# Left sums three steps earlier, and a softmax's exps moved within the last batch of a graph layer

## The chip, the cores and the metric

The kernel runs on one core of a Trainium2 chip. The metric is the device time of one execution in microseconds; the median of several runs counts. The core has five engines with queues of their own: TensorE (PE, matrix products), VectorE (DVE), ScalarE (ACT), GpSimd (POOL) and SyncE (SP), which here issues the DMAs.

## The reference

Sixteen graphs (batches) of 1024 nodes with 512 features pass through two layers over one 1024 x 1024 matrix adj. Cut to what matters:

```python
# layer 0
h = relu(layernorm(x))
x = x + (adj @ h) @ W0 + bias
# layer 1, graph attention
u = relu(layernorm(x)); h = u @ W
e = leaky_relu(s1[:, :, None] + s2[:, None, :]) * adj   # s1 = h.a1, s2 = h.a2
att = softmax(e, axis=2)
x = x + elu(att @ h + beta * h)
```

Everything is float32. The kernel takes s1 and s2 straight from u, with the vectors W.a1 and W.a2.

## The kernel before

**Products.** Each large product is done as a 2 x 2 block product with seven block products instead of eight, p1 to p7 (table `PRODUCTS`), with sums of blocks on both sides. In layer 0, from batch 1 on, six of the seven (all but p7) are split once more in the same way, into seven inner products r1 to r7 of half the size: 128 x 128 weights, 256 columns moving. `products_a2` writes out the order by hand. An inner product needs sums of its left operand: `inner_left` makes them on DVE with four adds of 128 x 256. The first of them (`s[:, 0]`) is the weight of r5, the second of r6, the fourth of r3; the third add changes the operand in place for r7. In the trace these sums are `in_p`, the operands `h` and `hS`, and the outputs `y_p3y`, `y_p3x` (the inner banks of p3) and `y_Y`, `y_X`, `y_W` (the outer PSUM banks). ACT copies r1, r5 and r7 out of PSUM, DVE adds r6 and then the whole to the outer bank (`y_p5t`, `y_p3t` and so on are these temporaries).

**Steps.** The order around this is a plan by hand. A batch of layer 0 is cut into steps: 0 to 6 hold p1 with p2, 7 to 13 p6 with p5, 14 to 20 p3 with the plain p7, 21 to 27 p4 with the first of the products with W0 (`po_Y`). Then `layer0_b` runs the other products with W0 with its own step numbers, two for each product, 2 to 13. After each step the plan's calls for that step are recorded, and every engine executes its own instructions strictly in the order in which they were recorded. Beside the products of batch b the plan does the norm of batch b + 1 (`h_stats`, `h_relu`) and what follows batch b − 1: its second norm (`o.stats`, `o.relu`), the stores of x (`x1d`) and u (`ud`), and `o.logits`, two multiply-and-sum instructions on DVE for each 128 rows of u. `o.store_logits` ends with a small DVE transpose of s2 over a tile `s2t` that POOL first clears. `load_res` fetches the residual rows (`xr`) for the current batch.

**The first softmax.** Batch 0's attention for layer 1 is begun inside layer 0. In batches 5 to 12 the masked logits are made, one row block g at a time, and stored to DRAM (`ed`). In the last batch of layer 0 (b = 15) they come back and are finished, by two plans of letters, `FIRST_A` (steps 0 to 27) and `FIRST_B` (steps of `layer0_b`): `Rg` reloads block g (512 KB, tile `er`), `Eg` takes its exp on ACT in four instructions, `Vg` turns it on DVE in two block transposes, `B` and `b` take buffers for the result, `S` and `s` send the sums through DRAM to all partitions (`sd`, `sall`), `D` and `d` put the diagonal in, `T1` and `T2` are block sums for layer 1's products. Steps 0 and 1 of the second plan are run at steps 23 and 26 of the first.

**Buffers.** Pool `b4` has 12 slots of 4 KB per partition. The inner sums, the temporaries, the outer sums, `er` and `e` tiles all live there. Pool `stat` gives two slots to most tags; PSUM has eight banks.

All engine calls go through the class `InOrder`, so every instruction of the profile has its line, L115; tiles tell them apart.

Of the kernel before, what the change touches and what calls it, by code (L numbers as in the profile page):

```python
# [29 lines left out]
F32 = mybir.dt.float32  # L30
# [4 lines left out]
P = 128  # L35
Q = 32
# [29 lines left out]
def kernel(  # L66
# [12 lines left out]
    B, N, D = x.shape  # L79
# [14 lines left out]
    stat = ctx.enter_context(tc.tile_pool(name="stat", bufs=2))  # L94
# [12 lines left out]
    class InOrder:  # L107


        def __init__(self, engine):  # L110
            self.engine = engine
# [5 lines left out]
    pe, dve, act, pool, sp = (  # L117
        InOrder(e) for e in (nc.tensor, nc.vector, nc.scalar, nc.gpsimd, nc.sync)
    )
# [217 lines left out]
    class Weighted:  # L337
# [9 lines left out]
        def steps(self, n, left):  # L347

            prod, _, bn, kind, first, last = self.products[n]

            def step(q, i, dc):
                if first and i == 0 and dc == 0:
                    self.banks[kind, q] = bank(f"{self.name}_{kind}{q}")
                ps = self.banks[kind, q].rearrange("p (i o) -> p i o", i=2)
                pe.matmul(
                    ps[:, i, :], left[:, dc, ts(2 * q + i, P)], self.w[:, W_BLOCK[bn], dc, :],
                    start=(first and i == 0 and dc == 0), stop=(last and dc == 1),
                    skip_group_check=True,
                )
                if i and dc:  # L360
                    self.done(prod, q, ps)

            return [partial(step, q, i, dc) for q in range(2) for i in range(2) for dc in range(2)]
# [261 lines left out]
    class LayerOut:  # L625
# [3 lines left out]
        def __init__(self, b):  # L629
            self.b = b  # L630
            self.us = {}
            self.norms = {}
            x1d[b] = dram.tile([2, 2, P, 2 * D], F32, name=f"x1d_{b}")
            names = ("U00", "U01", "U10", "U11")
            ud[b] = {n: dram.tile([P, 1024], F32, name=f"ud_{b}_{n}") for n in names}
            s1d[b] = dram.tile([P, NCH], F32, name=f"s1d_{b}")
            s2d[b] = dram.tile([G, Q * Q], F32, name=f"s2d_{b}")
            self.s12 = stat.tile([P, 2, NCH], F32, tag="s12", name=f"s12_{b}")

        def keep(self, nh, q):  # L640
            xr = xrs[self.b, nh, q]
            sp.dma_start(out=x1d[self.b][nh, q], in_=xr.rearrange("p k d -> p (k d)"))
# [27 lines left out]
        def store_logits(self):  # L670

            b = self.b
            sp.dma_start(out=s1d[b], in_=self.s12[:, 0, :])
            s2t = stat.tile([P, 2, Q], F32, tag="s2t", name=f"s2t_{b}")
            pool.memset(s2t[:, 0, :], 0.0)
            dve.tensor_copy(s2t[:, 0, 0:NCH], self.s12[:, 1, :])
            dve.transpose(s2t[:, 1, :], s2t[:, 0, :])
            sp.dma_start(out=s2d[b].rearrange("s (g q) -> (s g) q", q=Q), in_=s2t[:, 1, :])
# [426 lines left out]
    def plan_out(o, b):  # L1105

        return steps(
            (-1, o.keep, 0, 1), (-1, o.keep, 1, 0), (-1, o.keep, 1, 1), (0, o.stats, 0, 1, 0),
            (1, o.stats, 1, 0, 0), (2, o.relu, 0, 0), (3, o.stats, 1, 0, 1),
            (4, o.stats, 0, 1, 1), (7, o.relu, 1, 0), (8, o.relu, 0, 1), (9, o.stats, 1, 1, 0),  # L1110
            (10, o.stats, 1, 1, 1), (11, o.relu, 1, 1),
            (3, o.store, 0, 0), (8, o.store, 1, 0), (9, o.store, 0, 1), (12, o.store, 1, 1),
            (0, inner_left, b, "p6"), (1, inner_left, b, "p5"),
            (3, o.logits, 0, 0, 0), (4, o.logits, 0, 0, 1), (8, o.logits, 1, 0, 0),
            (9, o.logits, 1, 0, 1), (10, o.logits, 0, 1, 0), (11, o.logits, 0, 1, 1),
            (13, inner_left, b, "p3"), (15, o.logits, 1, 1, 0), (16, o.logits, 1, 1, 1),
            (16, o.store_logits), (18, inner_left, b, "p4"),
            (10, load_res, b, 0, 0), (13, load_res, b, 0, 1), (15, load_res, b, 1, 0),
            (18, load_res, b, 1, 1),
        )  # L1120
# [28 lines left out]
    def plan_softmax(order, s):  # L1149
# [35 lines left out]
        13: {9: "N n"},  # L1185
    }
    FIRST_A = {
        1: "R0", 4: "R1", 7: "B E0 V0 R2", 10: "E1 V1 R3", 12: "R4", 15: "E2 V2", 18: "b R5",
        22: "R6",
    }  # L1190
    FIRST_B = {
        0: "E3 V3 S", 1: "E4 V4 R7", 3: "E5 V5", 4: "E6 V6", 6: "E7 V7 s", 7: "D", 9: "T1a",
        10: "T1b", 11: "d", 12: "T2a", 13: "T2b",
    }
    LOADS_U = {5: ("U00",), 7: ("U01",), 9: ("U10", "U11")}

# [2 lines left out]
    out_of = None  # L1199
    for b in range(B):  # L1200
        plans = [plan_out(out_of, b)] if b else []
        plans_b = [plan_bias(b)]
        if b + 1 < B:
# [105 lines left out]
```

## Time and profile before

| | us |
|---|---|
| three runs | 2328.81, 2331.11, 2330.7 |
| their median | 2330.7 |
| the profiled execution | 2327.41 |
| its span, first to last instruction | 2325.6 |

The profile is of one execution, and its durations are summed against that execution's own 2327.41 us. The chain of waits that ended last lies for 81% on PE:

```profile
PE 81%; ACT 7%; DVE 7%; DMA 3%; issue 2%; SPq 1%; POOL 0%; DVEq 0%; ACTq 0%; POOLq 0%
```

Layer 0 takes the first half: its last products with W0 end at 1155.7 us. In a row of waits stand the engine and the tile it was to write, what it waited for, the total in us, the number of times and the longest. In a timeline row stand the start, the time until the last of a merged group ended (matmuls overlap, so that this is longer than the step to the next start), the engine, the operation and the tiles. The work of the reloaded blocks, from the view of the tile er (least, median and longest duration in ns, first and last start in us):

```profile
L115 ACT ACTIVATE er<-er,nm x32: 492/495/514, 1094.5 to 1144.6; 128x256 f32<-128x256 f32 x32
L115 DVE STREAM_TRANSPOSE pT<-er x16: 669/684/712, 1096.6 to 1145.8; 128x512 f32<-128x512 f32 x16
```

That is 32 exps of some 495 ns on ACT and sixteen block transposes of some 684 ns on DVE, between 1094.5 and 1146.5 us.

### The profile page before, as it was taken

The page shows a single profiled execution, that of the slowest core. Times are in us where ns is not written, and L with a number is a line of the kernel's source. Part 1 is how long each engine was busy: PE and PEld are TensorE (multiplying, and loading weights), DVE is VectorE, ACT ScalarE, POOL GpSimd, SP SyncE. Part 2 cuts the span into 40 slices and gives each one's busy share as a digit, 9 for nine tenths or more (in the row PEclk, how much of TensorE's full clock was granted, in tenths as well). Part 3 has the DMA queues.
Part 4 walks back from the last instruction along what each step waited for, and adds up shares of the span by engine and source line. Part 5 has one row for each costly group of instructions (what it writes and reads, how often), then busy time and mean ns, then how long its engine had stood idle before and what let it go on. Part 6 is the DMA issues. An engine that isn't in the chain of part 4 may idle for free.

```text
span 2325.6 us, 29418 instructions
## 1 busy us (share of the span) xinstructions
PE 2276.7 (98%) x8344; PEld 1587.3 (68%) x8344; DVE 1865.1 (80%) x4101; ACT 1544.3 (66%) x4147; POOL 529.3 (23%) x680
## 2 busy tenths in 40 slices
PE   9999999999999999999999999999999999999998
PEld 5787778877778877788755666556665466655565
DVE  7877787887888877877988788888988888878774
ACT  3766667666776667676367767677676776767753
POOL 1332222332232323122101222022220122201220
PEclk9999999999999999999999999999999999999999
DMA  6334343343343343433554545555456443455441
GB/s 213 126 129 150 123 155 122 135 137 121 134 158 128 125 144 111 145 126 122 173 168 146 164 135 168 183 162 166 138 167 190 154 155 115 147 186 160 136 128 37
DMA packets 194291, 336.02 MB, mean 144 GB/s; under 512 B 78800, under 2 KB 86992, under 8 KB 194128
## 3 DMA queue, kind: packets, MB, share of 16 engines
q1 hardware_dynamic: 193808, 333.61, 44.1%
q8 instruction: 66, 1.08, 0.2%
q14 instruction: 97, 0.79, 0.1%
q10 hardware_dynamic: 320, 0.52, 0.1%
HBM read 228.33 MB, written 109.91 MB: 145 GB/s over the span
## 4 chain that ended last, share of the span: by engine, by line
PE 81%; ACT 7%; DVE 7%; DMA 3%; issue 2%; SPq 1%; POOL 0%; DVEq 0%; ACTq 0%; POOLq 0%
PE z_Y L115 15%; PE y_Y L115 10%; PE po_Y L115 10%; PE pq_Y L115 8%; PE z_X L115 7%; PE po_X L115 5%; PE pq_X L115 4%; PE z_W L115 4%; PE y_W L115 3%; ACT xr L115 2%; PE po_W L115 2%; PE y_X L115 2%; PE pq_W L115 2%; ACT junk L115 2%; PE y_p1y L115 2%; PE y_p4y L115 2%
## 5 line engine op out<-in xcount | busy, mean ns | idle before, releaser
L115 POOL TENSOR_TENSOR x<-x,r 128x512 f32<-128x512 f32 x120 | 198.9, 1674 | 883.7 <-DVE x L115 325.3
L115 ACT ACTIVATE e<-e,nm 128x256 f32<-128x256 f32 x480 | 237.2, 498 | 140.5 <-DVE nm L115 140.5
L115 DVE CUSTOM_DVE_ANT_0 e<-e,mask 128x256 f32<-128x256 f32 x512 | 226.4, 498 | 105.8 <-DMA mask<-maskd 88.3
L115 PE MATMUL z_Y<-pT,ul_U 128*128 128x512 f32 x512 | 224.9, 592 | 0.0
L115 ACT ACTIVATE e<-s2b,s1b 128x256 f32<-128x256 f32 x512 | 216.5, 501 | 0.0
L115 POOL TENSOR_TENSOR xr<-xr,bias_bc 128x512 f32<-128x512 f32 x128 | 163.1, 1295 | 222.6 <-DVE xr L115 190.1
L115 PE MATMUL po_Y<-w_c,y_C 128*128 128x256 f32 x768 | 188.3, 379 | 0.0
L115 PEld LDWEIGHTS z_Y<-pT,ul_U 128*128 128x128 f32 x512 | 97.4, 190 | 115.5 <-issue 110.4
L115 PE MATMUL pq_Y<-w_c,z_C 128*128 128x256 f32 x768 | 174.4, 380 | 0.4 <-ACT z L115 0.4
L115 DVE CUSTOM_DVE_ANT_0 junk<-xr,v_bc 128x512 f32<-128x512 f32 x240 | 166.0, 692 | 6.8
L115 PEld LDWEIGHTS pq_Y<-w_c,z_C 128*128 128x128 f32 x768 | 145.6, 190 | 28.3 <-issue 7.6
L115 PE MATMUL y_Y<-adjT_B,h 128*128 128x512 f32 (+1 forms) x332 | 160.1, 596 | 1.6 <-ACT adjT_B L115 1.6
L115 PEld LDWEIGHTS po_Y<-w_c,y_C 128*128 128x128 f32 x768 | 146.1, 190 | 20.1 <-issue 0.5
L115 DVE STREAM_TRANSPOSE pT<-e 128x512 f32<-128x512 f32 x240 | 155.6, 687 | 1.0
L115 ACT ACTIVATE h<-x,nb_h,r_h 128x512 f32<-128x512 f32 (+1 forms) x132 | 98.2, 792 | 50.5 <-POOL nb_h L115 50.4
L115 ACT ACTIVATE junk<-xr 128x512 f32<-128x512 f32 x120 | 75.6, 630 | 70.4 <-DVE xr L115 69.9
L115 PE MATMUL po_X<-w_c,y_S 128*128 128x256 f32 x512 | 115.7, 379 | 0.0
L115 PE MATMUL pq_X<-w_c,z_S 128*128 128x256 f32 x512 | 115.6, 379 | 0.0
L115 PE MATMUL z_Y<-pT_T,ul_U 128*128 128x512 f32 x256 | 113.3, 594 | 2.1 <-DVE pT_T L115 1.9
L115 PE MATMUL z_W<-pT,ul_U 128*128 128x512 f32 x256 | 112.5, 592 | 0.0
L115 PE MATMUL z_Y<-pT_T,ul_S 128*128 128x512 f32 x256 | 112.5, 592 | 0.0
L115 PE MATMUL z_X<-pT_T,ul_S 128*128 128x512 f32 x256 | 112.5, 592 | 0.0
(227 smaller groups left out, 5056.0 us busy)
## 6 DMA issues: line engine op xcount, KB each, us to landing
mask<-maskd SPq DMA_DIRECT2D x128, 512.0 KB
x<-in_x_dram SPq DMA_DIRECT2D x64, 512.0 KB
xr<-in_x_dram SPq DMA_DIRECT2D x256, 128.0 KB
x1d<-xr SPq DMA_DIRECT2D x64, 512.0 KB
ul_U<-ud_U SPq DMA_DIRECT2D x64, 512.0 KB
x<-x1d SPq DMA_DIRECT2D x64, 512.0 KB
out_dram<-x SPq DMA_DIRECT2D x252, 128.0 KB
ud_U<-xr SPq DMA_DIRECT2D x60, 512.0 KB
```

The source lines that it names most:

```text
L115: return lambda *args, **kwargs: tc.keep_in_program_order(f(*args, **kwargs))
```

## The change

`inner_left` of p3 is called after step 10 instead of 13, and the logits that stood at 10 and 11 go to 12 and 13. The tile `s2t` is taken, and cleared by POOL, when the batch's `LayerOut` object is made instead of in `store_logits`. `FIRST_A` and `FIRST_B` get other steps: the reloads begin at step 11 instead of 1, the exps at 14 instead of 7, and the last five blocks come from step 22 on. The sum over blocks 0 to 3 (`S`) goes from step 23 to 24, that over 4 to 7 (`s`) stays at 6 of the second plan; `D` and the block sums `T1a` to `T2b` come one or two steps earlier.

```diff
@@ LayerOut.__init__ @@
             self.s12 = stat.tile([P, 2, NCH], F32, tag="s12", name=f"s12_{b}")
+            self.s2t = stat.tile([P, 2, Q], F32, tag="s2t", name=f"s2t_{b}")
+            pool.memset(self.s2t[:, 0, :], 0.0)
@@ LayerOut.store_logits @@
             sp.dma_start(out=s1d[b], in_=self.s12[:, 0, :])
-            s2t = stat.tile([P, 2, Q], F32, tag="s2t", name=f"s2t_{b}")
-            pool.memset(s2t[:, 0, :], 0.0)
+            s2t = self.s2t
             dve.tensor_copy(s2t[:, 0, 0:NCH], self.s12[:, 1, :])
@@ plan_out @@
             (3, o.logits, 0, 0, 0), (4, o.logits, 0, 0, 1), (8, o.logits, 1, 0, 0),
-            (9, o.logits, 1, 0, 1), (10, o.logits, 0, 1, 0), (11, o.logits, 0, 1, 1),
-            (13, inner_left, b, "p3"), (15, o.logits, 1, 1, 0), (16, o.logits, 1, 1, 1),
+            (9, o.logits, 1, 0, 1), (10, inner_left, b, "p3"), (12, o.logits, 0, 1, 0),
+            (13, o.logits, 0, 1, 1), (15, o.logits, 1, 1, 0), (16, o.logits, 1, 1, 1),
             (16, o.store_logits), (18, inner_left, b, "p4"),
@@ plans of the first softmax @@
     FIRST_A = {
-        1: "R0", 4: "R1", 7: "B E0 V0 R2", 10: "E1 V1 R3", 12: "R4", 15: "E2 V2", 18: "b R5",
-        22: "R6",
+        11: "R0", 12: "R1", 14: "B E0", 15: "V0 R2", 16: "E1", 17: "V1 E2", 18: "V2", 20: "b R3",
+        22: "E3", 23: "V3 R4", 24: "S", 25: "E4", 26: "V4 R5",
     }
     FIRST_B = {
-        0: "E3 V3 S", 1: "E4 V4 R7", 3: "E5 V5", 4: "E6 V6", 6: "E7 V7 s", 7: "D", 9: "T1a",
-        10: "T1b", 11: "d", 12: "T2a", 13: "T2b",
+        2: "E5 R6", 3: "V5 E6 R7", 4: "V6", 5: "E7", 6: "V7 s D", 7: "T1a", 8: "T1b", 11: "d T2a",
+        12: "T2b",
     }
```

## The prediction

> **What bounds the kernel now.** I read the page's busy shares, the waits of TensorE (PE), the waits of VectorE (DVE), then the timeline and the windows of the one place that the waits name. First the page:
>
> ```profile
> PE 2276.7 (98%) x8344; PEld 1587.3 (68%) x8344; DVE 1865.1 (80%) x4101; ACT 1544.3 (66%) x4147; POOL 529.3 (23%) x680
> ```
>
> PE is the bound; only 2325.6 − 2276.7 = 48.9 us of the span has it idle. Its waits, then the two of DVE's that matter:
>
> ```profile
> PE y_p3x L115 <- DVE in_p L115: 28.4, 15, 2.0
> PE y_p5y L115 <- DVE y_p5t L115: 4.6, 1, 4.6
> ```
> ```profile
> DVE s2t L115 <- POOL s2t L115: 38.3, 15, 3.0
> ...
> DVE y_X L115 <- ACT y_p5t L115: 13.9, 15, 0.9
> ```
>
> The reader is to see one wait, y_p3x on in_p, once in each of the 15 batches that use inner products, and one of 4.6 us that occurs once. PE's timeline in one such batch:
>
> ```profile
> 607.58 1.03 PE L115 MATMUL y_p3y<-adjT_B,hS 128*128 128x256 f32 x4
> 610.62 1.14 PE L115 MATMUL y_p3x<-ext,in_p 128*128 128x256 f32 x4 [2.02 <-DVE in_p L115]
> 611.56 3.58 PE L115 MATMUL y_Y<-adjT_B,h 128*128 128x512 f32 x4
> 614.98 1.03 PE L115 MATMUL y_X<-ext,hS 128*128 128x256 f32 x4
> ```
>
> The starts count. Undisturbed, four 128x256 matmuls take 0.865 us and the four of y_Y 1.72. From p3y to y_Y are 3.98 us where 1.73 are due: 2.25 lost. From y_Y to y_X are 3.42 where 1.72 are due: another 1.70 lost, while PE counts as busy. The windows say why (PEclk is the third value from the right):
>
> ```profile
> 607.00:611.00 4.00, 1.98 (x10) 1.46 (x9) 3.04 (x8) 3.22 (x7) 0.00 (x0) 1.00 0.53 188
> 611.00:615.00 4.00, 4.00 (x9) 1.86 (x8) 3.31 (x10) 3.11 (x11) 0.00 (x0) 0.57 0.89 206
> 615.00:619.00 4.00, 4.00 (x16) 2.79 (x15) 1.19 (x4) 3.87 (x13) 1.13 (x4) 1.00 0.06 9
> ```
>
> After the gap the clock falls to half for some 3.4 us. The steps between successive y_p3x starts show how often: 69.55 us without, 71.25 with. From 116.97 to 1036.47 there are 13 steps, 919.5 us in all = 13 × 69.55 + 9 × 1.70: 9 of 14 batches pay it. So the wait costs more than the 28.4 us of its row.
>
> Why in_p is late, on DVE:
>
> ```profile
> 607.24 0.69 DVE L115 TENSOR_TENSOR y_Y<-y_Y,y_p6t 128x512 f32<-128x512 f32 x1
> 608.85 1.30 DVE L115 TENSOR_TENSOR y_X<-y_X,y_p5t 128x512 f32<-128x512 f32 x2 [0.93 <-ACT y_p5t L115]
> 610.06 0.42 DVE L115 TENSOR_TENSOR in_p<-hS 128x256 f32<-128x256 f32 x1
> ...
> 616.99 0.17 DVE L115 COPY s2t<-s 128x8 f32<-128x8 f32 x1 [2.57 <-POOL s2t L115]
> ```
>
> in_p stands behind both y_X adds, which wait for ScalarE (ACT).
>
> **What the Trainium skill says.** "TensorE: Matmul & The Clock Gate", "What's actually happening": the array's clock runs full or half, decided by activity in a free-running window of about 3.4 us. The trace agrees in factor, length and in that only some gaps are hit; it disagrees in that the page wants an idle window, whereas gaps of 2.02 us suffice here. The trace decides. The same page, "Architectural detail": ACT and DVE are strict FIFO; the trace agrees (in_p behind y_X), so moved work must be checked by what is queued behind it. "Trainium Kernel Development and Optimization", "Key Constraints": all queues' DMAs share 16 engines; the reload er_7, issued at 1137.36 behind two ul loads, lets its exp start only at 1143.08.
>
> **The change part by part.**
>
> *Left sums of p3 (15 batches).* No instruction is added. In DVE's order the four adds of in_p take the place of the logits of (0,1,0) ahead of y_p5t: 610.06 to 611.52 = 1.46 us against 602.78 to 604.14 = 1.36. So y_p5t, y_p6t and y_Y keep their times within 0.1. In the built program in_p waits on no buffer, and p3x no longer on DVE. Saved in each of batches 1 to 14: 2.25 us; 14 × 2.25 = 31.5. The half-clock stretches go with their cause: 9 × 1.70 = 15.3.
>
> *What is late next.* I moved PE's starts in this batch 3.95 us earlier and followed the queues. The logits now stand after y_X (ends 610.06): three pairs at 1.46 reach 614.4, s2t 614.8, y_p3t reads its bank by 615.2. PE's next matmuls on that bank come at 616.2: 1.0 us spare. y_X of p3 needs ACT's copy, done by 610.15, PE comes at 611.02: 0.9 spare. ACT has its four norm sums (6.7 us) and a relu before the second y_p3t copy, now done at 620.0, 2.8 us after PE; DVE's y_X adds and sums then end at 626.1, y_p4t at 626.5, while PE's overwrite is at 627.4: 0.9 spare. ACT's idle stretches in p4 (2.5 and 5.2 us) absorb the lag, and by po_X all engines stand to PE as before. DVE is busy 57.2 us of a 71.25 us batch, so 67.3 hold it. Taken: 0 new wait; bounds 0 and 1 us per batch.
>
> *s2t earlier.* POOL's memset moves to the start of the batch; a POOL op of 0.12 us in an idle stretch. DVE's stall of 38.3 / 15 = 2.55 us is off PE's path now, so I count 0 for it, but it is cover for the first part: with it, y_p3t would end near 617.2 and PE would wait 1.0 us, 14 us in all.
>
> *The first softmax in batch 15.* From the p6 to the p4 starts are 1125.45 − 1090.89 = 34.56 us; undisturbed pieces of other batches add up to 12.08 (666.75 to 678.83) + 1.73 + 11.18 (1037.41 to 1048.59) = 24.99. So 9.57 us are lost now: 4.65 for y_p5t behind the exps and turns of er_0 and er_1, 0.5 for y_p5t's copy, the rest mostly at half clock (0.55 granted from 1107 to 1114). In the new order both turns leave the stretch before y_p5t, so that one runs as in other batches and p3y can start at 1102.98 (1090.89 + 12.08). I then placed each queue on that time:
>
> ACT: er_0 to er_2 (step 14 on) fill the place of the norm sums, which this batch lacks: 3 × 1.97 = 5.9 us for 6.7, from 1106.8 to 1112.7, in time for the second y_p3t copy (PE done 1112.6). Their reloads, 512 KB each, pass behind ud stores and xr loads on SP: er_0 can be issued by 1101.5 at the latest and er_1 at 1103.8, after the store that waits for a relu; about 4 us later they are there, er_1 (needed 1108.8) with least to spare.
>
> DVE: y_X ends at 1105.5, two logit pairs 1108.4, er_0's turn 1110.1 (1.30, and er_0's exps end at 1108.8), a pair 1111.55, s2t 1111.95, y_p3t 1112.35; PE is due at its bank at 1111.6: wait 0.8. Two more turns and p4's sums later DVE ends p3's sums at 1123.5; er_3's turn comes ahead of y_p4t, which reads its bank by 1125.2, PE due at 1123.7: wait 1.5.
>
> SP: er_5 to er_7 now stand behind sd_0, which waits for er_3's last exp (about 1121.4), the sall loads (4.4 us after sd now) and two more ul loads. From 1128.5 there are 5 × 0.5 MB queued; at the 350 GB/s of the busiest slices here they land at about 1134.5, 1136 and 1137.5. Their turns stand ahead of the xr adds that free the po banks: waits of 0.2, 0.4 and 1.0 us.
>
> Sum of waits 3.9; saved 9.57 − 3.9 = 5.6 (rounded down). Bounds: 9.5 with no new wait, −4 if the reloads come 10 us later. What is late next there: sd_1 follows er_7's exps, so the next softmax's s1b and s2b loads end near layer 1's first product instead of 3 us before it; ACT takes z_W first and DVE reaches the masks later, so no PE wait. T2, needed 13.7 us into layer 1, is ready some 6 us before.
>
> *Sum*, against the profiled execution's own 2327.4 us: 31.5 + 15.3 + 5.6 = 52.4, giving 2275.0. The median of the runs, 2330.7, is 3.3 above it, about what two more half-clock stretches would be; as these should vanish, I take no correction: 2275.
>
> **The rivals.**
>
> *New waits in p3 and p4.* The three margins of 0.9 to 1.0 us rest on one batch; if one is short by 1 us everywhere: 2275 + 14 = 2289. Against: PE has no other repeated wait now.
>
> *The half clock stays.* If it were not the gap that triggers it: 2275 + 15.3 = 2290. Against: I find it only beside a wait.
>
> *The tail of batch 15.* Reloads stacked behind sd_0 cost 10 us more, PE idle and once at half clock: 2287. For: they are issued later by whole steps, with 2.5 MB queued in one go.
>
> *The wait stays*, because p3x also waits for a bank or ACT: 2327. Against: its one other wait is on PE itself.
>
> *Slower.* in_p's four adds now stand ahead of y_p5t, whose read PE needs at 605.85 while it ends at 604.56: 1.3 us spare. Anything that holds the first add (a b4 buffer not yet free at step 10, where C12, C22 and three sums share 12) is a PE wait beyond 1.3. It decides when the hold passes 3.3 us: 2.0 of wait and 1.7 at half clock in 14 batches are the 52.4 gained. At 6 us: 14 × (4.7 + 1.7) − 52.4 = +37, so 2365. For: in the order of the built program another store's wait has moved onto the first add of p6's sums. Against: no semaphore on that add.
>
> **How the numbers follow.** Forecast 0.62; new waits 0.12; half clock 0.06; tail 0.14; wait stays 0.02; slower 0.04. The likeliest alone spans 2268 to 2281 (batch 15 from +9.5 to 0, runs within about 2). With the three rivals of the same sign: 2268 to 2291, which leaves out about a tenth. A difference of 0.2% (4.7 us) is about what a measurement can tell. Faster 0.94, same 0.02, slower 0.04.
>
> **What would show it.** Right: no y_p3x row among PE's waits; y_p3x steps of 67.3 us; PEclk 1.00 through p3; DVE's s2t row gone; in batch 15 PE waits of 1 to 2 us at p3y and p4y instead of 4.65 at p5y. Wrong: a y_p3y, y_X or y_p4y row 14 times; half clock without a gap; long PE waits on po banks after 1125.

## The result, and the profile after

| | before | after |
|---|---|---|
| median of 4 runs each, us | 2329.76 | 2276.76 |
| lowest and highest, us | 2326.34, 2331.11 | 2274.24, 2277.8 |
| the profiled execution, us | 2327.41 | 2277.24 |
| its span, us | 2325.6 | 2275.2 |

The changed kernel takes 0.9773 of the time (95% interval 0.9756 to 0.979), 53.0 us less. 2275.0 had been forecast, with a range of 2268 to 2291.

First the page of the changed kernel, its busy shares:

```profile
PE 2254.3 (99%) x8344; PEld 1578.3 (69%) x8344; DVE 1863.5 (82%) x4101; ACT 1540.7 (68%) x4147; POOL 526.6 (23%) x680
```

PE is now idle for 2275.2 − 2254.3 = 20.9 us of the span; it was 48.9. Its busy time also fell, by 22.4 us, with the same 8344 matmuls: matmuls at half clock count as busy, and 15.3 us of it are the nine stretches behind p3x. Next two rows of PE's waits (total, times, longest), and one of DVE's:

```profile
PE y_p4y L115 <- DVE y_p4t L115: 1.6, 1, 1.6
PE y_p3y L115 <- DVE y_p3t L115: 1.5, 1, 1.5
```
```profile
DVE y_p3t L115 <- ACT y_p3t L115: 35.8, 14, 2.6
```

The row of y_p3x on in_p, 15 times 2.0, is gone, and so are y_p5y's 4.6 and DVE's 38.3 us at s2t. From batch 1 to the end of layer 0 PE keeps only the two single waits shown, both in batch 15. DVE has a new repeated wait, for ACT's second copy of p3, which no PE row answers to. The timeline of PE in the batch that corresponds to the one shown before:

```profile
586.52 1.03 PE L115 MATMUL y_p3y<-adjT_B,hS 128*128 128x256 f32 x4
587.39 1.03 PE L115 MATMUL y_p3x<-ext,in_p 128*128 128x256 f32 x4
588.25 1.88 PE L115 MATMUL y_Y<-adjT_B,h 128*128 128x512 f32 x4
589.97 1.03 PE L115 MATMUL y_X<-ext,hS 128*128 128x256 f32 x4
```

The starts are 0.87, 0.86 and 1.72 apart: no idle time and full speed. The window of the same stretch has PE busy throughout, at a granted clock (third value from the right) of 1.00:

```profile
587.00:591.00 4.00, 4.00 (x16) 2.79 (x15) 3.22 (x9) 3.19 (x9) 0.00 (x0) 1.00 0.74 226
```

From batch 1 to batch 14 the 13 steps between successive y_p3x starts are 67.30 us (one is 67.35). They took 919.5 us before and take 991.24 − 116.29 = 874.95 now. The difference, 44.55, is 13 × 2.25 + 9 × 1.70 to the hundredth.

### The profile page after: what moved, and what is told of

The parts are those of the page before. It is cut to its first block, busy times and chain, and to the rows that moved or that the text cites. A ratio compares the mean times of both kernels' runs of the same rounds, so it can differ in the third digit from the quotient of the medians.

```text
span 2275.2 us, 29359 instructions
## 1 busy us (share of the span) xinstructions
PE 2254.3 (99%) x8344; PEld 1578.3 (69%) x8344; DVE 1863.5 (82%) x4101; ACT 1540.7 (68%) x4147; POOL 526.6 (23%) x680
## 4 chain that ended last, share of the span: by engine, by line
PE 86%; DVE 5%; DMA 4%; ACT 2%; SPq 1%; issue 1%; POOL 0%; DVEq 0%; ACTq 0%; POOLq 0%
PE z_Y L115 15%; PE y_Y L115 11%; PE po_Y L115 10%; PE pq_Y L115 8%; PE z_X L115 7%; PE po_X L115 5%; PE y_X L115 5%; PE pq_X L115 4%; PE z_W L115 4%; PE y_W L115 3%; PE po_W L115 2%; PE pq_W L115 2%; PE y_p1y L115 2%; PE y_p5y L115 2%; PE y_p6y L115 2%; PE y_p2y L115 2%
## 5 line engine op out<-in xcount | busy, mean ns | idle before, releaser
L115 PE MATMUL y_Y<-adjT_B,h 128*128 128x512 f32 (+1 forms) x332 | 147.2, 554 | 0.9 <-DVE adjT_B L115 0.9
L115 PE MATMUL z_X<-pT,ul_S 128*128 128x512 f32 x256 | 112.5, 592 | 0.0
```

Of the source, the lines that this page charges most:

```text
L115: return lambda *args, **kwargs: tc.keep_in_program_order(f(*args, **kwargs))
```

## The experiments

Each run was timed against the kernel before on the same chip. "Layer 0" in the text is the stretch from batch 1's first y_p3y to layer 1's first product, z_Y; it is 1041.8 us in the kernel before and 989.0 in the changed one. What comes after it scattered from 1167 to 1176 us over the profiles of all these kernels and by 3.0 between two profiles of the changed kernel itself, so a few us are read from layer 0 and not from the median; layer 0 differs by 1.1 between those two profiles.

### The sums put back

```diff
-            (9, o.logits, 1, 0, 1), (10, inner_left, b, "p3"), (12, o.logits, 0, 1, 0),
-            (13, o.logits, 0, 1, 1), (15, o.logits, 1, 1, 0), (16, o.logits, 1, 1, 1),
+            (9, o.logits, 1, 0, 1), (10, o.logits, 0, 1, 0), (11, o.logits, 0, 1, 1),
+            (13, inner_left, b, "p3"), (15, o.logits, 1, 1, 0), (16, o.logits, 1, 1, 1),
```

> The changed kernel with one part undone: p3's left sums are called after step 13 again and the two logits after 10 and 11; the early s2t and the new plan of the first softmax stay. Theory (the late sums cost an idle gap and the half clock behind it): the y_p3x row on in_p is back, 14 or 15 times about 2.0 us, steps between y_p3x starts of 69.5 and 71.2 us, granted clock about 0.98 over layer 0, time 2276.8 + 15 x 2.25 + about 9 x 1.7 = 2326 (2318 to 2331). Rival 1 (half clock is not caused by the gap): steps of 69.5 only, 2276.8 + 33.8 = 2311. Rival 2 (the gain came from the early s2t or the softmax): 2277 to 2290.

Measured: 2324.87, ratio 0.9979 (0.9972 to 0.9985). From PE's waits:

```profile
PE y_p3x L115 <- DVE in_p L115: 30.3, 15, 2.0
```

Ten of the 14 steps are about 71.25 us and four 69.55, as in the kernel before. Putting the sums back costs 48 of the 53 us, and the half clock comes back with the gap. Both rivals fall.

### The sums alone

The kernel before with the plan lines of the sums changed as in the diff of the change, and nothing else.

> The kernel before with one part of the change alone: p3's left sums after step 10, the logits after 12 and 13; s2t is cleared late and the first softmax keeps its old plan. Theory: -31.5 for the waits, -15.3 for the half clock, +9 to +14 for a new y_p3y wait of 0.65 to 1.0 us in 14 batches behind the late s2t; batch 15 unchanged or up to 2 us better: 2329.8 - 46.8 + 9 to 14 = 2292 to 2297. Rival (the parts simply add, s2t is worth nothing): 2283. Rival (the sums are worth nothing without the early s2t): 2310 or more.

Measured: 2297.33, ratio 0.9853 (0.9836 to 0.9869), 0.3 above the range expected. No half-clock stretch in batches 1 to 14; steps of 68.07 us where 67.30 are reached with the early s2t. PE's row at y_p3y is 7.0 us over 14 times, 0.5 each, and another 0.27 go with each restart.

### The clearing put back

```diff
 LayerOut.__init__
-            self.s2t = stat.tile([P, 2, Q], F32, tag="s2t", name=f"s2t_{b}")
-            pool.memset(self.s2t[:, 0, :], 0.0)
 LayerOut.store_logits
-            s2t = self.s2t
+            s2t = stat.tile([P, 2, Q], F32, tag="s2t", name=f"s2t_{b}")
+            pool.memset(s2t[:, 0, :], 0.0)
```

> The changed kernel with the tile s2t taken and cleared in store_logits again; sums early and new softmax stay. Theory (the early clearing is cover for the early sums): DVE's s2t row is back with about 2.5 us, y_p3t ends some 2.4 us later, and PE, which has 1.1 us to spare at p3y's bank in the changed kernel, waits 0.65 to 1.4 us there in 14 batches, without half clock: 2286 to 2296. Rival A (the stall stays hidden): 2277. Rival B (PE takes the whole stall, or the stall brings half clock): 14 x 2.5 = 35 or more, 2312 and up.

Measured: 2290.14, ratio 0.983 (0.9814 to 0.9846); steps of 68.08, so 0.78 lost in each of 14 batches, 10.9 in all, and no half clock. The other 2.5 us of the median are open: in the profile layer 1 is 4.4 us longer than in the changed kernel's, where 3.0 is scatter. The timeline of one batch shows the chain (POOL, DVE, PE):

```profile
599.98 0.20 POOL L115 TENSOR_TENSOR nb_h<-mv_h,r_h 128x2 f32<-128x2 f32 x1
600.11 0.12 POOL L115 MEMSET s2t<- 128x32 f32 x1
600.27 0.17 DVE L115 COPY s2t<-s 128x8 f32<-128x8 f32 x1 [1.72 <-POOL s2t L115]
...
601.04 1.13 PE L115 MATMUL y_p3y<-adjT_B,hS 128*128 128x256 f32 x4 [0.52 <-DVE y_p3t L115]
```

A memset of 0.12 us stands in POOL's queue behind the norm's small operations, which wait for ACT; DVE waits for it, and y_p3t and PE's bank behind DVE. In the kernel before, DVE's stall of 2.55 us held up no product (PE has no y_p3y row there), and the run with the sums put back shows the early clearing saving nothing there: its steps are 69.55 and 71.25 us again, with s2t cleared early. It pays only together with the early sums, as cover.

### The old softmax plan put back

`FIRST_A` and `FIRST_B` as before the change, all else changed.

> The changed kernel with the old plan of the first softmax; sums early and early s2t stay. Theory: batch 15 loses 9.6 us again where it now loses 3.05, so +6.5, 2283 (2280 to 2286), with a y_p5y wait on y_p5t of about 4.6 us once and a p6-to-p4 stretch of about 34 us; less if part of the 9.6 came from the late sums of that batch. Rival (the new plan is worth nothing by itself): 2277 or less.

Measured: 2281.93, ratio 0.9796 (0.9782 to 0.9811): 5.2 us above the changed kernel. PE's wait at y_p5y is back with 4.7 us, and the granted clock is 0.50 from 1058.3 to 1065.1 us. Layer 0 is 993.9 against 989.0.

The medians in a row, from several chips on which the kernel before took 2329.8 to 2330.9: 2297.33 with the sums alone, 2281.93 with the early clearing too, 2276.76 with the softmax.

### How early the sums must be

```diff
-            (9, o.logits, 1, 0, 1), (10, inner_left, b, "p3"), (12, o.logits, 0, 1, 0),
-            (13, o.logits, 0, 1, 1), (15, o.logits, 1, 1, 0), (16, o.logits, 1, 1, 1),
+            (9, o.logits, 1, 0, 1), (10, o.logits, 0, 1, 0), (11, o.logits, 0, 1, 1),
+            (12, inner_left, b, "p3"), (15, o.logits, 1, 1, 0), (16, o.logits, 1, 1, 1),
```

> The changed kernel with p3's left sums after step 12 instead of 10 and the logits after 10 and 11 again: one step earlier than in the kernel before, just ahead of the two y_X adds instead of just behind them. Theory (only the place behind the y_X adds, which wait for ScalarE, makes the sums late): in_p's first add ends within 0.1 us of the time PE needs it; 2277 (2275 to 2281), no half clock. Rival (three steps are needed): a y_p3x wait of 1 us or more in 14 batches, 2291 or more, with the half clock up to 2310.

Measured: 2278.11, ratio 0.9781 (0.9764 to 0.9797); steps of 67.35, 0.05 above those of the changed kernel. One step is enough. What made the sums late was their place behind two y_X adds that wait for ACT, not DVE's load.

### How long a gap must be for the half clock

The same, with additional adds on a scratch tile ahead of the sums; the second run has eight where the first has four. They write nothing that is read. Their medians rest on two executions each.

```diff
+    def hold():
+        j = junk(1)
+        for _ in range(4):
+            add(j[:, 0:256], j[:, 256:512], j[:, 0:256])
...
+            (12, hold), (12, inner_left, b, "p3"), (15, o.logits, 1, 1, 0), (16, o.logits, 1, 1, 1),
```

> Sums of p3 after step 12, as in the run of that name, with four additional 128 x 256 adds on a scratch tile ahead of them on DVE; the outputs are as before. It makes a wait of PE of about 1.5 us (4 x 0.36) at p3x in each batch, shorter than the 2.02 us of the kernel before. Theory (a gap triggers the half clock only if it leaves half or more of a free-running 3.4 us stretch idle; 9 of 14 hits at 2.02 us put the bound near 1.6 us): no half clock, steps of 67.3 + 1.5 = 68.8 us only, 2277 + 15 x 1.5 = 2299. Rival (any gap of PE triggers, with a chance that grows with its length): some 5 of 14 steps 1.7 us longer, 2308 or more.

> The same with eight additional adds, for a wait of about 2.9 us in each batch. Theory (bound near 1.6 us idle in a free-running stretch of 3.4 us): a hit in about 12 of 14 batches, steps mostly 67.3 + 2.9 + 1.7 = 71.9 us, 2277 + 15 x 2.9 + 12 x 1.7 = 2341. Rival (the chance of a hit does not depend on the gap's length above a minimum): 9 of 14 again, 2336. Rival (only an idle stretch of 3.4 us counts): none, 2321.

Measured: 2304.18, ratio 0.9886 (0.9866 to 0.9906), with four adds; 2360.68, ratio 1.0129 (1.0108 to 1.0149), with eight. PE's timeline around p3x with four, then with eight:

```profile
600.34 1.10 PE L115 MATMUL y_p3x<-ext,in_p 128*128 128x256 f32 x4 [1.51 <-DVE in_p L115]
601.28 1.88 PE L115 MATMUL y_Y<-adjT_B,h 128*128 128x512 f32 x4
602.99 1.03 PE L115 MATMUL y_X<-ext,hS 128*128 128x256 f32 x4
```
```profile
264.35 2.05 PE L115 MATMUL y_p3x<-ext,in_p 128*128 128x256 f32 x4 [3.35 <-DVE in_p L115]
266.19 3.62 PE L115 MATMUL y_Y<-adjT_B,h 128*128 128x512 f32 x4
```

With 1.51 us idle y_Y takes its undisturbed 1.71 us in every one of batches 1 to 14; steps are 69.06. With 3.35 idle it is slow in all of them. By idle time of the gap, batches 1 to 14:

| idle, us | batches with a half-clock stretch |
|---|---|
| 1.51 (four adds) | 0 of 14 |
| 2.02 (kernel before; sums put back) | 9 of 14; 10 of 14 |
| 3.35 (eight adds) | 14 of 14 |

Each gap costs 0.23 to 0.25 us more than its idle time (69.06 − 67.30 = 1.76 for 1.51). Of this, some 0.16 is how idle time is counted: from the end of the last group, 1.03 us after its start, where the next would have started after 0.865. With four adds the run is 5 us above its expectation: 15 restarts of 0.25, and a half-clock stretch in batch 15, where the gap is 2.55. With eight it is 20 us above: the gap is longer than foreseen (3.35 for 2.9), and five of the 14 batches lost 2.8 to 3.1 us at half clock instead of 1.4 to 1.7. Both rivals of the second expectation (hits independent of length; only a gap of 3.4 us counts) fall with the table.

The length of a gap is not yet the rule. The traces hold the time of every change of the granted clock. In the nine profiles with more than one change, all 95 changes lie within 0.003 us of a grid of 3.413 us that runs on through the whole kernel, each profile with its own start; in the kernel before, the half-clock stretches of batches 1 to 14 begin 21 or 41 times 3.413 us apart. So PE's idle time, as the profile shows it, can be added up window by window of this grid, from batch 1 on, over all 13 profiles:

| clock in a window | PE idle in it, us | windows | the next window |
|---|---|---|---|
| full | up to 1.85 | 8174 | full in all |
| full | 2.00 to 3.41 | 40 | half in all |
| half | up to 0.62 | 40 | full in all |
| half | 0.64 to 2.01 | 10 | half again in all |

In the kernel before, the five gaps of 2.02 us that brought no half clock are cut by the edge of a window: no more than 1.62 to 1.67 us of them lie in one. The nine that did bring it lie whole in one. The expectations' bound, about half a window or 1.6 us, is therefore too low. The gap shown above, on its own grid:

```profile
260.27:263.68 3.41, 0.73 (x4) 0.30 (x2) 3.17 (x9) 0.95 (x3) 0.00 (x0) 1.00 0.69 234
263.68:267.09 3.41, 2.74 (x6) 1.90 (x7) 3.38 (x9) 1.11 (x3) 0.00 (x0) 0.50 0.92 224
267.10:270.51 3.41, 3.41 (x7) 1.68 (x6) 2.51 (x10) 3.28 (x12) 0.00 (x0) 0.50 0.05 8
```

PE (first value after the comma) is idle for 2.7 us of the first window, so the second is at half clock; the rest of the gap, 0.67 us, falls into the second, so the third is at half clock too. That is what the five costlier batches have in common.

### Batch 15: what the two remaining waits hang on

In the profiled execution of the changed kernel the wait at p3y was 1.48 us where 0.8 had been foreseen. POOL, DVE and PE around it:

```profile
1065.92 1.37 POOL L115 TENSOR_TENSOR xr<-xr,bias_bc 128x512 f32<-128x512 f32 x1 [8.03 <-DMA xr<-in_x_dram]
...
1066.22 1.11 DVE L115 COPY s2t<-s 128x8 f32<-128x8 f32 x1
...
1067.93 1.13 PE L115 MATMUL y_p3y<-adjT_B,hS 128*128 128x256 f32 x4 [1.48 <-DVE y_p3t L115]
```

The copy of eight numbers per partition takes 1.11 us; its median is 0.17. It ends at 1067.33, 0.04 after POOL's add, and y_p3t follows it on DVE. The Trainium skill, "SBUF — State Buffer", section "Who interferes with whom", says that a VectorE copy can take the port pair that it shares with GpSimd, and that whichever comes second waits until the first has finished. The traces agree: in all 13 profiles together four of these copies began while an add of POOL was running; each took 1.04 to 1.11 us and ended within 0.04 us of that add, and no other took over 0.3. Another add of POOL stretches a multiply-and-sum of DVE some 9 us earlier, to 1.69 us for 0.69; this is so in all profiles of this section (1.64 to 1.78), and no run removes it. Three runs were made on one chip:

```diff
 LayerOut.logit_parts
-                    op0=ALU.mult, op1=ALU.add, accum_out=self.s12[:, i, g : g + 1],
+                    op0=ALU.mult, op1=ALU.add, accum_out=self.s12[:, 0, g : g + 1] if i == 0 else self.s2t[:, 0, g : g + 1],
 LayerOut.store_logits
-            dve.tensor_copy(s2t[:, 0, 0:NCH], self.s12[:, 1, :])
```

> The changed kernel, but the logits of s2 are accumulated into the tile s2t itself and DVE's copy from s to s2t is gone; nothing else moves. Theory (the copy took 1.11 us instead of 0.17 in batch 15 because it was locked out by a 1.37 us add of POOL that had begun just before; the transpose and y_p3t that follow read one SBUF operand each and are not locked out): PE's wait at p3y in batch 15 falls from 1.48 to 0.2 to 0.5 us, the wait at p4y stays at 1.0 to 1.6; 2275.7, a difference that only the trace can show. Rival (the long copy is something else, or the lock moves to the next DVE instruction): the transpose or y_p3t starts 1 us late and the wait stays at 1.2 us or more.

```diff
 FIRST_A, in addition
-        11: "R0", 12: "R1", 14: "B E0", 15: "V0 R2", 16: "E1", 17: "V1 E2", 18: "V2", 20: "b R3",
-        22: "E3", 23: "V3 R4", 24: "S", 25: "E4", 26: "V4 R5",
+        11: "R0", 12: "R1", 14: "B E0", 15: "R2", 16: "E1", 17: "V0 V1 E2", 18: "V2", 20: "b R3",
+        22: "E3", 23: "R4", 24: "S V3", 25: "E4", 26: "V4 R5",
```

> The same, and two turns of the first softmax are put behind the adds that PE waits for: er_0's turn from step 15 to 17, er_3's from 23 to 24; the reloads keep their steps. Theory (the two remaining waits of batch 15 are these turns): no y_p3y and no y_p4y wait over 0.3 us, 2276.8 - 3.05 = 2273.7. Rival (DVE is full in this stretch, so a wait only moves to another bank or to p4's sums): PE's waits between p6 and the end of layer 0 still add up to 1.5 us or more, 2275.3 or above.

> The changed kernel once more, on the same chip as the two runs above: 2276.8 (2274 to 2279), waits of about 1.5 us at p3y and 1.0 to 1.6 us at p4y in batch 15.

| run | median, us | ratio and interval | PE waits p6 to p4 of batch 15 | layer 0, us |
|---|---|---|---|---|
| changed kernel, first profile | 2276.76 | 0.9773 (0.9756 to 0.979) | 1.48 + 1.57 | 989.0 |
| changed kernel again (after_again) | 2277.88 | 0.9784 (0.9771 to 0.9798) | 0.63 + 1.31 + 2.01 | 990.1 |
| copy gone (direct) | 2277.94 | 0.9784 (0.977 to 0.9797) | 0.28 + 1.53 + 2.01 | 990.0 |
| copy gone, turns later (direct_turns) | 2276.59 | 0.978 (0.9767 to 0.9793) | 2.00 + 0.68, and half clock | 991.6 |

The first expectation holds for the wait at p3y (0.28) and misses the rest: 2.01 us at p4y and 1.53 at y_Y, so that the waits add up to 3.8 us, between the 3.05 and 3.95 of the two profiles of the changed kernel, and nothing is gained. In the repeated run of the changed kernel the copy happened to start first:

```profile
1065.19 0.17 DVE L115 COPY s2t<-s 128x8 f32<-128x8 f32 x1
1065.27 1.27 POOL L115 TENSOR_TENSOR xr<-xr,bias_bc 128x512 f32<-128x512 f32 x1 [8.40 <-DVE s L115]
```

There it took 0.17 us, and PE waited 0.63 at p3y, then 1.31 for y_C and 2.01 for y_p4t. With the turns moved there is no wait at p3y, but PE loses the time elsewhere, as the rival said that it would. PE after that change:

```profile
1076.65 1.13 PE L115 MATMUL y_Y<-adjT_T,h 128*128 128x256 f32 x4 [2.00 <-DVE y_C L115]
...
1079.03 2.07 PE L115 MATMUL y_p4y<-adjT_T,h 128*128 128x256 f32 x4 [0.68 <-DVE y_p4t L115]
```

That the clock fell here is a matter of where the wait lay: these 2.00 us are whole in one window, and the 0.68 behind them kept the next one at half; in the two other runs the waits of 1.31 or 1.53 and 2.01 us are cut by window edges (1.85 at most in one), and the clock stayed full. What the three runs have in common is one line of ACT, here with the turns moved:

```profile
1068.77 0.51 ACT L115 ACTIVATE er<-er,nm 128x256 f32<-128x256 f32 x1 [4.79 <-DMA er<-ed]
...
1070.75 0.35 ACT L115 COPY y_p3t<-y_p3y 128x256 f32<-128x256 f32 x1
```

ACT waits 4.79 us for the reload of er_2, and its second copy of p3 stands behind the four exps, and with it p3's second sums on DVE. On DVE er_2's turn, which waits for the same exps, stands ahead of these sums as well.

### The exps behind the copy

```diff
 FIRST_A, against the run with the turns later
-        11: "R0", 12: "R1", 14: "B E0", 15: "R2", 16: "E1", 17: "V0 V1 E2", 18: "V2", 20: "b R3",
-        22: "E3", 23: "R4", 24: "S V3", 25: "E4", 26: "V4 R5",
+        11: "R0", 12: "R1", 14: "B E0", 15: "R2", 16: "E1", 17: "V0 V1", 19: "E2", 20: "b R3",
+        22: "E3", 23: "R4", 24: "S V2 V3", 25: "E4", 26: "V4 R5",
```

> As direct_turns, and er_2's exps go from step 17 to 19, behind ScalarE's second copy of p3, and er_2's turn from 18 to 24, behind y_p4t. Theory (what PE still lost in batch 15, 2.0 + 0.7 us and a half-clock stretch in direct_turns, 3.95 us in the repeated run of the changed kernel, was ScalarE waiting up to 4.8 us for er_2's reload with p3's second copy, and so all of p3's sums, behind it): no PE wait over 0.3 us from p6 of batch 15 to the end of layer 0, first z_Y some 3 to 4 us earlier after the batch's start, 2273 to 2274.5. Rival (the reload of er_4 or the sums that follow take its place): waits of 1.5 us or more at y_p4y or the po banks, 2275.5 or above.

Measured: 2275.24, ratio 0.9767 (0.9754 to 0.978), 0.7 above the range expected and 0.3 below the rival's. No PE wait between p6 and the po banks; there two of 0.27 and 0.26 us. ACT and PE, from the timeline:

```profile
1066.88 0.37 ACT L115 COPY y_p3t<-y_p3y 128x256 f32<-128x256 f32 x1 [1.77 <-PE y_p3y L115]
1069.13 0.51 ACT L115 ACTIVATE er<-er,nm 128x256 f32<-128x256 f32 x1 [1.88 <-DMA er<-ed]
```

The copy now waits for PE alone and the exps wait for the reload with nothing urgent behind them. Layer 0 takes 986.7 us, 2.3 and 3.4 less than in the two profiles of the changed kernel. The intervals of the ratios overlap, so the trace shows this gain and the medians don't settle it. The run moves er_2's exps and its turn together, so it doesn't tell which of the two held up p3's sums.

## Why the prediction was right

**The wait at p3x, 31.5.** Measured to the hundredth of a step: 2.25 in each of the 13 steps, and in batch 1 y_Y starts 1.73 us after y_p3y instead of 3.98, the same 2.25 less. The reason was the right one: one step earlier, ahead of the y_X adds, gives the same.

**The half clock, 15.3.** 9 × 1.70, gone with the gap; the sums put back brought it back. That a gap of 2.02 us suffices was right; the forecast did not need to know that what counts is how much of a gap falls into one window. The rival in which it stays is refuted. So are the two in which PE goes on waiting at p3x: in_p's first add was held by nothing, and no y_p3x row is left.

**No new wait in p3 and p4.** None in batches 1 to 14. The margins had been put at 0.9 to 1.0 us: in the batch shown, y_p3t has read its bank by 594.07 with PE due at 595.13, 1.1 spare, and y_p4t by 605.73 with PE due at 606.34, 0.6 spare. DVE's wait for ACT's second copy came as worked out (the row of 14 × 2.6).

**s2t as cover, 0 by itself and about 1.0 us in 14 batches if missing.** The size was 0.78 and the total 10.9 over these batches for 14 foreseen. The mis-sized term is DVE's stall: the forecast let it hold y_p3t from 615.2 to 617.2, and in the shifted batch it is 1.72 us.

**Batch 15, 5.6.** Layer 0 became 52.8 us shorter, of which 44.55 + 2.25 belong to batches 1 to 14; 6.0 remain. The terms were less exact than their sum. The wait at p3y was 1.48 for 0.8 in one profile, where POOL locked out the copy, and 0.63 in the other; neither this nor the stretched multiply-and-sum is in the forecast. The one at p4y was 1.57 and 2.01 for 1.5. The waits at the po banks, 1.6 in the forecast, didn't come at all. What was missed is er_2: the forecast placed its exps from 1110.7 to 1112.7 on the times of before, with no wait for its reload, and found them "in time for the second y_p3t copy". In the changed kernel ACT waited 3.95 us for its reload, with that copy behind. This is what the last run removed. So the 5.6 came out near 6.0 in part by luck: waits at the po banks that didn't come made up for waits that were larger. In the repeated profile layer 0 is 1.1 us longer, and 4.8 remain.

**The sum.** 52.4 foreseen, 50.4 in the span: 52.8 in layer 0, less 1.5 that batch 1 began later and 0.9 in layer 1, both of the size by which repeated profiles differ. That the median of before lay 3.3 above its profiled execution and needed no correction also held: the medians differ by 53.0. Whether two more half-clock stretches made up the 3.3, the reason given, was not tested.

## What to carry to other kernels

When PE is 98% busy, look at the step between successive starts of the same product, not at the idle time: a wait of 2.0 us cost 3.95 in most batches, of which the wait row shows half. In a strict queue, find what the late instruction stands behind (here two adds that wait for another engine) and move it just past that; two steps further brought 0.05 us per batch here. And where an operation waits for a reload, ask which urgent copy stands behind it on the same engine before counting its wait as hidden.

## What the runs showed of the hardware

- From batch 1 on, the granted clock fell to half after each of 40 windows of 3.413 us in which PE was idle for 2.00 us or more, and after none of 8174 with 1.85 or less. The Trainium skill, "TensorE: Matmul & The Clock Gate", section "What's actually happening", says that the window runs freely and is about 3.4 us long, which the grid bears out, and that the clock falls after an idle window, which isn't needed here. In the first 12 us of the kernel, where PE turns adj, two windows don't fit (1.60 us idle and half clock after it, 1.94 and full).
- A window at half clock is followed by another when PE was idle for 0.64 us or more of it (10 of 10), and by full clock at 0.62 or less (40 of 40). So a second short wait right behind a long one can double the price, as the 0.68 us did in the run with the turns moved later (0.50 granted from 1078.0 to 1084.8 us).
- A restart after a gap costs 0.23 to 0.27 us beyond the idle time that the profile shows.
- A DVE copy of 128 x 8 took 1.11 us when POOL's add had begun 0.3 us ahead of it, and 0.17 when it began 0.08 ahead of POOL's. A shift of 0.4 us between the two queues decides, so the same kernel's two profiles have PE waits of 1.48 and 0.63 us at this place. The small transpose and y_p3t that ran inside POOL's add in the second profile were not longer (0.21 and 0.38 us in both).
